# Scan pass of a state-space and attention kernel: a fourth exp buffer, other queue ranks, two states handed over

## The chip, the cores and the metric

The kernel runs on one core of one Trainium2 chip. The metric is the time of one launch on the device in microseconds (us). Its engines work side by side: TensorE (PE, with its weight loads as PEld), VectorE (DVE), ScalarE (ACT), GpSimd (POOL), and SyncE (SP), which here only issues DMAs.

## What is computed

Input x has 8 batches of 64 x 64 positions with 96 channels. A first layer normalizes groups of channels, projects to 2 x 192 channels, convolves one half (3 x 3 by channel, then silu), and runs a selective scan over the 4096 positions in four directions; the result is normalized, gated and projected back. A linear attention and a small quantized feed-forward layer follow. The change touches the selective scan alone:

```python
def step(h, inps):
    d_t, u_t, b_t, c_t = inps
    h = h * jnp.exp(d_t[..., None] * A) + (d_t * u_t)[..., None] * b_t[:, :, None, :]
    y = jnp.einsum('bkdn,bkn->bkd', h, c_t)
    return (h, y)
h0 = jnp.zeros(u.shape[:3] + (A.shape[-1],), u.dtype)
_, ys = jax.lax.scan(step, h0, (dT, uT, BT, CT))
```

For every batch b, direction k (4) and channel d (192) there are 16 states n, each of them a first-order recurrence over 4096 positions, with factor exp(delta A) and addend (delta u) B. The output is the sum over n of h C.

## The kernel before

There are three passes: `pass1` (normalization, projection, convolution, the projections that give delta, B and C), `pass2` (the scans), and `pass3` (all the rest). Intermediate results lie in DRAM between them. The change is in `pass2`, lines 541 to 864.

**Tiling of the scan pass.** Batches go in 4 pairs. The 2 x 192 channels of a pair make three chunks of 128 partitions: chunks 0 and 1 hold 128 channels of one batch each (one-batch chunks, c below 2), and chunk 2 holds the last 64 channels of both (the mixed chunk). Each chunk runs through 4 directions k, and each direction in 4 pieces of 1024 positions (backward for k of 2 and 3). That makes 4 x 3 x 4 x 4 = 192 pieces, each with 16 states: 3072 scans.

**What one piece needs.** `prepare` loads the split factors (`xdt`, `xb`) and `u`, turns B so that it can scale by partition (`bT`), makes `delta` by a softplus on ScalarE, `du` = delta u on GpSimd, and its transpose `duT`. Three of these steps hold a buffer of `wide` (PSUM) for a while. Then for each state n:

- `decay`: ScalarE computes `da` = exp(delta A), 128 x 1024.
- The addend reaches PSUM (`wide`) in one of three ways, chosen by `WAYS` on line 55. ScalarE's way (`scaled`): ScalarE multiplies the 8 blocks of `duT` by B into `x`, in 8 instructions (16 in the mixed chunk), and PE transposes them into `wide`. GpSimd's way (`scaled_by_pool`): the same product in one or two instructions into `xg`. VectorE's way (the rest of the states): PE broadcasts B into `wide` and VectorE multiplies `wide` by `du` in place.
- `scan`: VectorE runs the recurrence over 1024 positions into `h`, which holds two states.
- For each pair of states: `load_c` loads C, broadcast over the partitions, into `c`; `times_c` multiplies `c` by `h` on GpSimd; `sum_over_n` adds the product into `acc` (PSUM) by 16 PE transposes; `carries` copies the last position for the next piece.
- `take_acc` copies `acc` out once all 16 states are in.

**Order.** `weave` (line 142) fixes the order of the instructions on every engine before anything runs. Each unit of work is a generator that yields the engine that it needs next, an estimated cost and a delay, and at times a buffer that must be free. `weave` takes, step after step, the unit that could begin first; among those that could begin at the same time, as is the rule on an engine with a queue, the smaller rank goes first. `add` sets the rank to `at * N + n - lead`: a unit with lead 5 counts as though it belonged five states earlier. `prep` has lead 8. The emitted order is then kept by the hardware's in-order queues, whatever the real times are: an instruction that waits holds up all behind it on its engine.

**Buffers.** `room` (line 550) gives the number of buffers of each kind: 6 of `c`, 3 of `da`, 3 of `h` (pairs of states), 3 of `x`, 3 of `wide`, one each of `xg`, `ud` and `acc`. A `Slots` object for each tells `weave` when the next becomes free by its own estimates. On the chip a semaphore makes the writer wait for it.

Of the kernel before, what the change touches and what calls it, by code (L numbers as in the profile page):

```python
# [51 lines left out]
NPC = L // T  # L52
NT = T // P

WAYS = [([2, 5, 6, 8, 11, 12, 14, 15], [3, 7]), ([2, 3, 7, 9, 14], [0, 5, 12])]
NS = 3

LATE = 5
# [9 lines left out]
def chunk_rows(pair, c):  # L68

    b0 = 2 * pair  # L70
    if c < 2:
        return [(slice(0, P), b0 + c, slice(0, P))]
    return [(slice(64 * j, 64 * j + 64), b0 + j, slice(P, DI)) for j in range(2)]
# [468 lines left out]
def pass2(ctx, tc, g, ident, engines, fixed, u_d, xd_d, b_d, dt_d, y_d):  # L542
# [4 lines left out]
    sp = InOrder(tc, nc.sync)  # L547
    one = ctx.enter_context(tc.tile_pool(name="p2one", bufs=1))
    two = ctx.enter_context(tc.tile_pool(name="p2two", bufs=2))
    room = {"c": 6, "da": 3, "h": 3, "x": 3, "wide": 3, "xg": 1, "ud": 1, "acc": 1}  # L550
    slots = {name: Slots(count) for name, count in room.items()}
    pools = {
        name: ctx.enter_context(tc.tile_pool(name=f"p2{name}", bufs=count, **({"space": PSUM} if name in ("wide", "acc") else {})))
# [7 lines left out]
    def take(name, shape, dtype=F32):  # L561

        return pools[name].tile(shape, dtype, name=name), slots[name].taken
# [79 lines left out]
    def load_c(at, m):  # L643
        pair, c, k, pc = pieces[at]
        parts = chunk_rows(pair, c)
        end = yield "sp", 0.5 * len(parts), 6.0, slots["c"]
        c2, slot = take("c", [P, 2, T])
        row = C0 + (k // 2) * N + 2 * m
        for part, b, _ in parts:
            rows = xd_d[b][k % 2][row : row + 2, pc * T : (pc + 1) * T]  # L650
            sp.dma_start(c2[part], rows.unsqueeze(0).to_broadcast([part.stop - part.start, 2, T]))
        made["c", at, m] = c2, slot
        done["c", at, m] = end

    def decay(at, n):

        _, c, k, _ = pieces[at]
        yield "delta", at
        end = yield "act", 1.06, 0.2, slots["da"]
        da, slot = take("da", [P, T])  # L660
        act.activation(da, made[at][2], AF.Exp, scale=a_neg[:, c // 2, k, n : n + 1])
        made["da", at, n] = da, slot
        done["da", at, n] = end

    def scaled(at, n):

        pair, c, _, _ = pieces[at]
        yield "duT", at
        x, (_, _, _, _, duT, bT) = None, made[at]
        for i in range(0, NT, 2):  # L670
            cost = 0.6 if c < 2 else 1.0
            end = yield ("act", cost, 0.2) if i else ("act", cost, 0.2, slots["x"])
            if i == 0:
                x, slot = take("x", [P, NT, P])
            for i2 in (i, i + 1):
                for j, (part, _, _) in enumerate(chunk_rows(pair, c)):
                    act.mul(x[:, i2, part], duT[:, i2, part], bT[:, i2, j * N + n : j * N + n + 1])
        made["x", at, n] = x, "x", slot
        done["x", at, n] = end

    def scaled_by_pool(at, n):
        pair, c, _, _ = pieces[at]
        yield "duT", at
        end = yield "pool", 2.0 if c < 2 else 2.2, 0.2, slots["xg"]
        x, slot = take("xg", [P, NT, P])
        _, _, _, _, duT, bT = made[at]
        for j, (part, _, _) in enumerate(chunk_rows(pair, c)):
            wide = part.stop - part.start
            b = bT[:, :, j * N + n : j * N + n + 1].to_broadcast([P, NT, wide])
            pool.tensor_mul(x[:, :, part], duT[:, :, part], b)  # L690
        made["x", at, n] = x, "xg", slot
        done["x", at, n] = end

    def products(at, n):

        pair, c, _, _ = pieces[at]
        by_act, by_pool = WAYS[c // 2]
        if n in by_act or n in by_pool:
            yield "x", at, n
            end = yield "pe", 1.3, 0.2, slots["wide"]  # L700
            dbu, slot = take("wide", [P, T])
            x, name, of_x = made["x", at, n]
            for i in range(NT):
                pe.transpose(dbu[:, i * P : (i + 1) * P], x[:, i, :], ident)
            slots[name].release(of_x, end)
        else:
            yield "du", at
            end = yield "pe", 0.7, 0.2, slots["wide"]
            dbu, slot = take("wide", [P, T])
            xb = made[at][0]  # L710
            for q in range(0, T, GRP):
                pe.matmul(dbu[:, q : q + GRP], spread(n, c), xb[:, q : q + GRP], start=True, stop=True)
            end = yield "dve", 1.22, 0.0
            dve.tensor_mul(dbu, made[at][3], dbu)
        made["dbu", at, n] = dbu, slot
        done["dbu", at, n] = end

    def scan(at, n):
        _, _, k, _ = pieces[at]
        rev, first = k >= 2, at % NPC == 0  # L720
        yield "dbu", at, n
        yield "da", at, n
        if not first:
            yield "carry", at - 1, n // 2
        if n % 2 == 0:
            end = yield "dve", 2.26, 0.2, slots["h"]
            made["h", at, n // 2] = take("h", [P, 2, T])
            done["begun", at, n // 2] = 0.0
        else:
            yield "begun", at, n // 2  # L730
            end = yield "dve", 2.26, 0.2
        h = made["h", at, n // 2][0][:, n % 2, :]
        (da, of_da), (dbu, of_dbu) = made["da", at, n], made["dbu", at, n]
        way = slice(None, None, -1) if rev else slice(None)
        init = 0.0 if first else carry[at // NPC][:, n : n + 1]
        dve.tensor_tensor_scan(h[:, way], da[:, way], dbu[:, way], init, ALU.mult, ALU.add)
        slots["da"].release(of_da, end)
        slots["wide"].release(of_dbu, end)
        one_more(("h", at, n // 2), 2, end)
        one_more(("scans", at), N, end)  # L740

    def carries(at, m):

        _, _, k, _ = pieces[at]
        yield "h", at, m
        end = yield "act", 0.12, 0.1
        if at // NPC not in carry:
            carry[at // NPC] = two.tile([P, N], F32, name="carry")
        h2, slot = made["h", at, m]
        last = 0 if k >= 2 else T - 1  # L750
        act.copy(carry[at // NPC][:, 2 * m : 2 * m + 2], h2[:, :, last])
        done["carry", at, m] = end
        one_more(("read", at, m), 2, end)
        if ("read", at, m) in done:
            slots["h"].release(slot, end)

    def times_c(at, m):
        yield "h", at, m
        yield "c", at, m
        end = yield "pool", 4.55, 0.2  # L760
        (h2, slot), (c2, _) = made["h", at, m], made["c", at, m]
        pool.tensor_mul(c2, c2, h2)
        done["term", at, m] = end
        if at % NPC == NPC - 1:
            slots["h"].release(slot, end)
            return
        one_more(("read", at, m), 2, end)
        if ("read", at, m) in done:
            slots["h"].release(slot, end)
# [42 lines left out]
    def take_acc(at):  # L812
        pair, c, k, pc = pieces[at]
        o = k % 2
        yield "sum", at
        end = yield "act", 0.95, 0.1
        if at % (K * NPC) == 0:
            for i in range(2):
                ys[i] = one.tile([P, NBLK, P], F32, name=f"y{i}")
        acc, slot = made["acc"]  # L820
        dst = ys[o][:, pc * NT : (pc + 1) * NT, :]
        act.copy(dst, acc)
        slots["acc"].release(slot, end)
        if k >= 2 and at % NPC == NPC - 1:
            yield "sp", 2.0, 6.0
            store_y(ys[o], o, chunk_rows(pair, c))
# [12 lines left out]
    for at, (pair, c, k, pc) in enumerate(pieces):  # L839
        by_act, by_pool = WAYS[c // 2]  # L840

        def add(kind, lead, unit, n=0):
            units.append((kind, at * N + n - lead, unit))

        add("prep", 8, prepare(at))
        for n in range(N):
            if n % 2 == 0:
                add("c", 12, load_c(at, n // 2), n)
            add("da", 2, decay(at, n), n)
            if n in by_act:  # L850
                add("x", 5, scaled(at, n), n)
            elif n in by_pool:
                add("xg", 4, scaled_by_pool(at, n), n)
            add("dbu", 1, products(at, n), n)
            add("scan", 0, scan(at, n), n)
            if n % 2 == 1:
                if at % NPC < NPC - 1:
                    add("carry", -2, carries(at, n // 2), n)
                add("term", 0, times_c(at, n // 2), n)
                add("sum", -4, sum_over_n(at, n // 2), n)  # L860
        add("acc", 0, take_acc(at), N)
# [289 lines left out]
```

## Time and profile before

| | |
|---|---|
| median of 3 runs | 10227.74 us (10223.3 to 10242.83) |
| the profiled execution's own time | 10238.11 us |
| its span, first to last instruction | 10236.3 us |
| first start and last end of the scans in it | 715.0 and 9321.7 us |
| VectorE busy over the span | 9578.9 us (94%) |
| GpSimd busy | 9194.7 us (90%) |
| ScalarE busy | 9152.3 us (89%) |
| products with C on GpSimd | 1536 x 4.555 us |
| mean granted TensorE clock | 0.895 |

The shares over the whole span mix three passes; the scan pass takes 84% of it. Lines of groups read: source line, engine, operation, output<-inputs with shapes and count, then busy us, mean ns of one, and the engine's idle time just before them with what ended it. Nearly all work goes through one helper, so the source line is L91 throughout and the tile names tell the groups apart: `x` are ScalarE's products, `da` the exps, `h` the scans, `wide` the PSUM buffers.

### The profile page before, as it was taken

The numbers are of one execution on the slowest core, as the hardware profiler recorded it, in microseconds if no ns is written. First come the engines' busy times: TensorE is split into PE (matmuls) and PEld (weight loads), VectorE is DVE, ScalarE is ACT, GpSimd is POOL, SyncE is SP. The second block draws the span as 40 slices with busy tenths as digits, with TensorE's granted clock in tenths as the row PEclk, the third lists the DMA queues.
The fourth block names the chain that finished last, engine by engine and source line by source line (L and its number), as shares of the span: only waits on it lengthen the run. The fifth ranks groups of instructions, "written<-read, shape, count | busy, mean of one in ns | idle before, by whom it ended". The sixth has DMA issues, their size and how long they took to land.

```text
span 10236.3 us, 152471 instructions
## 1 busy us (share of the span) xinstructions
PE 7669.6 (75%) x52384; PEld 6320.8 (62%) x52384; DVE 9578.9 (94%) x6886; ACT 9152.3 (89%) x20499; POOL 9194.7 (90%) x3280
## 2 busy tenths in 40 slices
PE   7767777776777777777777777777777777776887
PEld 3336666665666666666666666666666666565775
DVE  7969999999999999999999999999999999996776
ACT  5669999999999999999999999999999999995665
POOL 1449999999999999999999999999999999997886
PEclk8889989989998989989989999999999899997776
DMA  5766776689976766799866666999667668996442
GB/s 165 236 209 217 229 228 221 228 209 206 211 221 212 224 218 216 223 205 205 221 210 223 219 214 225 209 204 213 216 213 230 210 226 210 206 208 169 125 126 60
DMA packets 928006, 2103.29 MB, mean 205 GB/s; under 512 B 274475, under 2 KB 422732, under 8 KB 925698
## 3 DMA queue, kind: packets, MB, share of 16 engines
q1 hardware_dynamic: 924426, 2092.18, 72.3%
q8 instruction: 420, 6.88, 0.3%
q14 instruction: 352, 2.88, 0.1%
q0 software_dynamic: 432, 0.94, 0.0%
q10 hardware_dynamic: 2376, 0.40, 0.0%
HBM read 1917.59 MB, written 175.66 MB: 204 GB/s over the span
## 4 chain that ended last, share of the span: by engine, by line
DVE 28%; ACT 26%; issue 15%; PE 15%; POOL 12%; DMA 3%; SPq 1%; DVEq 0%; ACTq 0%; POOLq 0%
DVE h L91 20%; ACT x L91 10%; ACT da L91 10%; POOL c L91 8%; PE acc L91 6%; DVE wide L91 5%; PE wide L91 3%; ACT L91 2%; PE mm L91 2%; PE px L91 1%; ACT y L91 1%; POOL xg L91 1%; PE pa L91 1%; DMA xd_d<-xd 1%; ACT delta L91 1%
## 5 line engine op out<-in xcount | busy, mean ns | idle before, releaser
L91 POOL TENSOR_TENSOR c<-c,h 128x2048 f32<-128x2048 f32 x1536 | 6958.0, 4555 | 299.2 <-issue 135.9
L91 DVE TENSOR_TENSOR_SCAN h<-da,carry,wide 128x1024 f32<-128x1024 f32 x2304 | 5268.2, 2332 | 137.6 <-PE wide L91 34.4
L91 ACT ACTIVATE x<-duT,bT 128x128 f32<-128x128 f32 (+1 forms) x13312 | 3970.3, 368 | 2.0
L91 PE MATMUL acc<-ident,c 128*128 128x128 f32 x24576 | 3438.8, 298 | 573.1 <-POOL c L91 566.2
L91 ACT ACTIVATE da<-delta,a_neg 128x1024 f32<-128x1024 f32 x3072 | 3513.1, 1144 | 315.2 <-DVE h L91 302.3
L91 PEld LDWEIGHTS acc<-ident,c 128*128 128x128 f32 x24576 | 3122.8, 155 | 1008.2 <-POOL c L91 893.7
L91 PE MATMUL wide<-ident,x 128*128 128x128 f32 x10752 | 1559.8, 291 | 646.4 <-DVE h L91 587.9
L91 PEld LDWEIGHTS wide<-ident,x 128*128 128x128 f32 x10752 | 1307.2, 150 | 841.5 <-ACT x L91 397.4
L91 DVE TENSOR_TENSOR_SCAN h<-da,wide 128x1024 f32<-128x1024 f32 x768 | 1712.8, 2271 | 45.1 <-PE wide L91 13.9
L91 DVE TENSOR_TENSOR wide<-du,wide 128x1024 f32<-128x1024 f32 x1280 | 1544.2, 1208 | 39.8 <-PE wide L91 29.4
L91 PE MATMUL wide<-xb,sel 96*128 96x512 bf16 x2560 | 820.6, 404 | 696.0 <-DVE h L91 689.1
L91 POOL TENSOR_TENSOR xg<-duT,bT 128x512 f32<-128x512 f32 (+1 forms) x640 | 893.8, 1412 | 28.4 <-PE wide L91 15.3
L91 PEld LDWEIGHTS <-sel 96*128 96x128 bf16 x2560 | 232.8, 102 | 876.4 <-DVE h L91 625.9
L91 PE MATMUL wide<-ident,xg 128*128 128x128 f32 x3584 | 482.6, 279 | 119.0 <-DVE h L91 117.4
L91 PEld LDWEIGHTS wide<-ident,xg 128*128 128x128 f32 x3584 | 411.7, 144 | 148.7 <-issue 110.0
L91 ACT ACT_TABLE_LOAD x385 | 494.0, 1283 | 6.9
L91 POOL TENSOR_TENSOR du<-delta,u 128x1024 f32<-128x1024 f32 x192 | 457.3, 2382 | 7.7 <-DMA u<-u_d 7.7
L91 DVE SCALAR_TENSOR_TENSOR u<-xpad,conv_w,u 128x4096 f32<-128x4096 f32 x96 | 452.7, 4716 | 1.9
L91 PE MATMUL px<-u,w_xp 128*128 128x512 f32 x512 | 253.6, 636 | 61.9 <-ACT u L91 43.0
L91 PE MATMUL mm<-w_out,gt 128*128 128x96 f32 (+1 forms) x1024 | 268.3, 383 | 32.7 <-POOL gt L91 16.1
L91 ACT COPY y<-acc 128x1024 f32<-128x1024 f32 x192 | 192.5, 1003 | 84.5 <-PE acc L91 84.1
L91 POOL TENSOR_TENSOR bq<-bq,bs 128x512 f32<-128x512 f32 (+1 forms) x48 | 121.7, 2536 | 161.4 <-ACT bs L91 140.3
(136 smaller groups left out, 6285.6 us busy)
## 6 DMA issues: line engine op xcount, KB each, us to landing
c<-xd_d SPq DMA_DIRECT2D x1024, 1024.0 KB
c<-xd_d SPq DMA_DIRECT2D x1024, 512.0 KB
u<-u_d SPq DMA_DIRECT2D x127, 512.0 KB
xdt<-dt_d SPq DMA_DIRECT2D x1146, 36.0 KB
xb<-b_d SPq DMA_DIRECT2D x382, 96.0 KB
u<-u_d SPq DMA_DIRECT2D x128, 256.0 KB
y_d<-y SPq DMA_DIRECT2D x24, 1024.0 KB
y<-y_d SPq DMA_DIRECT2D x64, 384.0 KB
```

What stands on the lines that cost most here:

```text
L91: ins = getattr(self.engine, op)(*args, **kwargs).ins
```

## The change

Five values in the scan pass differ; no function is rewritten, and no instruction is added or dropped.

```diff
-WAYS = [([2, 5, 6, 8, 11, 12, 14, 15], [3, 7]), ([2, 3, 7, 9, 14], [0, 5, 12])]
+WAYS = [([2, 5, 6, 8, 10, 13, 14, 15], [3, 7]), ([2, 3, 7, 9, 14], [0, 5, 12])]
...
-    room = {"c": 6, "da": 3, "h": 3, "x": 3, "wide": 3, "xg": 1, "ud": 1, "acc": 1}
+    room = {"c": 6, "da": 4, "h": 3, "x": 3, "wide": 3, "xg": 1, "ud": 1, "acc": 1}
...
             if n % 2 == 0:
-                add("c", 12, load_c(at, n // 2), n)
-            add("da", 2, decay(at, n), n)
+                add("c", 8, load_c(at, n // 2), n)
+            add("da", 0, decay(at, n), n)
             if n in by_act:
-                add("x", 5, scaled(at, n), n)
+                add("x", 8, scaled(at, n), n)
             elif n in by_pool:
                 add("xg", 4, scaled_by_pool(at, n), n)
```

In the one-batch chunks ScalarE's way takes states 10 and 13 in place of 11 and 12, so VectorE's way takes 0, 1, 4, 9, 11, 12 in place of 0, 1, 4, 9, 10, 13. The mixed chunk keeps its split. `da` gets a fourth buffer of 128 x 1024 floats. In the order, loads of C count as 8 states early in place of 12, exps as 0 in place of 2, and ScalarE's products as 8 in place of 5.

## The prediction

> **What bounds the kernel now.** I first read the busy time of each engine by stage, then the waits of VectorE and of ScalarE inside the scan pass, then the groups of instructions, and last the timeline of one stall. The stages come from the first and last start of the scans, 715 us and 9322 us.
>
> The busy time by stage (columns: stretch and length, then busy us and count of PE, PEld, DVE, ACT, POOL, granted clock, DMA share, GB/s):
>
> ```profile
> 0.00:715.00 715.00, 521.22 (x1470) 246.82 (x1470) 548.06 (x244) 432.70 (x588) 231.28 (x110) 0.86 0.67 202
> 715.00:9322.00 8607.00, 6410.87 (x46792) 5484.31 (x46793) 8394.28 (x4351) 8193.57 (x18759) 8283.75 (x2403) 0.92 0.77 215
> 9322.00:10236.30 914.30, 737.48 (x4124) 589.72 (x4122) 636.57 (x2293) 526.00 (x1153) 679.65 (x769) 0.70 0.40 114
> ```
>
> All that the change touches lies in the middle row. There VectorE is busy 8394 of 8607 us (97.5%), GpSimd 96.2%, ScalarE 95.2%. VectorE is the bound, but with only 213 us of idle time, and two engines follow within 200 us. The gain is capped, and a loss is near.
>
> The waits of VectorE in that stage (who waited for whom, us in all, times, longest):
>
> ```profile
> DVE h L91 <- PE wide L91: 48.3, 48, 3.8
> DVE wide L91 <- PE wide L91: 29.4, 30, 1.1
> DVE h L91 <- POOL c L91: 5.3, 6, 1.2
> DVE h L91 <- ACT x L91: 4.6, 5, 2.5
> DVE h L91 <- ACT da L91: 2.1, 3, 1.1
> ```
>
> The long waits sum to some 91 us. The other 120 us are gaps of 0.11 us, 1038 of which stand where a scan follows directly on the multiplication that made its input. The reader is to see that exp (da) holds VectorE up for 2 us in all, so the fourth buffer removes next to no wait of the bound engine. Two thirds of the long waits are for PE. By VectorE's timeline 56 of the 91 us stand at states 9 to 12 of the one-batch chunks (c below 2), and only some 17 us in the mixed chunk.
>
> The waits of ScalarE in the same stage:
>
> ```profile
> ACT da L91 <- DVE h L91: 302.3, 530, 3.3
> ACT y L91 <- PE acc L91: 69.0, 99, 1.4
> ```
>
> ScalarE waits 302 us for a free exp buffer, that is for VectorE: it is often ahead as far as its buffers let it. That time is slack and no cost.
>
> The groups that price the parts (busy us, mean ns of one, idle before and its releasers):
>
> ```profile
> L91 DVE TENSOR_TENSOR_SCAN h<-da,carry,wide 128x1024 f32<-128x1024 f32 x2304 | 5268.2, 2332 | 137.6 <-PE wide L91 34.4
> L91 ACT ACTIVATE x<-duT,bT 128x128 f32<-128x128 f32 (+1 forms) x13312 | 3970.3, 368 | 2.0
> ...
> L91 ACT ACTIVATE da<-delta,a_neg 128x1024 f32<-128x1024 f32 x3072 | 3513.1, 1144 | 315.2 <-DVE h L91 302.3
> ...
> L91 DVE TENSOR_TENSOR wide<-du,wide 128x1024 f32<-128x1024 f32 x1280 | 1544.2, 1208 | 39.8 <-PE wide L91 29.4
> ...
> L91 ACT ACT_TABLE_LOAD x385 | 494.0, 1283 | 6.9
> ```
>
> One typical stall, on VectorE's timeline (start, length, idle before):
>
> ```profile
> 5927.54 2.29 DVE L91 TENSOR_TENSOR_SCAN h<-da,wide 128x1024 f32<-128x1024 f32 x1
> 5930.96 1.23 DVE L91 TENSOR_TENSOR wide<-du,wide 128x1024 f32<-128x1024 f32 x1 [1.13 <-PE wide L91]
> ```
>
> States 9 and 10 both go VectorE's way (broadcast by PE, multiplication, scan). At just this point the next piece's preparation holds one of the three PSUM buffers, so state 10's broadcast waits until state 9's scan has ended, and VectorE stands 1.13 us.
>
> **What the Trainium skill says.** "Perfetto Trace Analysis", section Optimization Strategy, has one look at the gaps of the saturated engine alone, and says that the same gap repeating there can mean too little SBUF or PSUM for the next tile. The 1.13 us gap, repeated at state 10 in some 20 pieces, agrees; but the buffer that is short is the PSUM one, and the change gives exp another. "ScalarE: Activation LUTs", section What ACT_TABLE_LOAD costs, gives about 1283 ns for a table load and an overlap of about 93 ns between ACTIVATEs. The trace agrees with both: 1283 ns, and products of 0.39 us that start 0.295 us apart. So ScalarE's costs in queue time are 8 x 0.295 = 2.4 us for one state's products in a one-batch chunk, 16 x 0.24 = 3.9 us in the mixed one, and 1.144 - 0.1 = 1.04 us for an exp.
>
> **The change, part by part.** Counts of instructions stay as they are: 8 states by ScalarE, 2 by GpSimd and 6 by VectorE in a one-batch chunk before and after, the same loads, the same PE work. Only order and buffers move.
>
> C's loads, lead 12 to 8: SP issues 8 times a piece and mostly waits for one of 6 buffers, so its order is set by when a buffer is free rather than by rank. The other loads of that queue are those of preparation (6 of xdt, 2 of xb, 1 or 2 of u), which could be taken sooner. No wait of VectorE or GpSimd names C's load with more than 5 us. I take 0, and plus or minus 20 us for the ends.
>
> Fourth exp buffer: it takes nothing off VectorE directly (2.1 us). It raises ScalarE's reserve by one exp, that is by one scan of 2.3 us (3.5 us with a multiplication). Cover for other losses, 0 by itself.
>
> Other states by ScalarE (10 and 13 in place of 11 and 12): the neighbouring pair on VectorE's way moves from 9, 10 to 11, 12. The pair's stall of 38 us (25 at state 10, 13 at state 12), with the rest of the 56 us, can go. What is late next is state 10's products: eight transposes by PE take 1.06 us where the broadcast took 0.6, and need the same PSUM buffer. If they wait for state 9's scan too, the stall is 1.3 us in place of 1.13. Also, 13, 14 and 15 are now three ScalarE states in a row: 3 x 2.4 = 7.2 us of products for 3 x 2.3 = 6.9 us of scans. I take half the 56 us as a gain of 28; the ends are -56 and +20.
>
> Ranks: before, products went ahead of an exp only when at most two states beyond it; now they do up to seven states beyond. So ScalarE fills all three product buffers before it returns to exps. Where exps are thinnest is measured: from the end of an exp to the start of its scan there are 4 to 6 us (median) at most states, but 0.8 to 1.2 us at state 12 of the one-batch chunks, just behind the softplus of the next piece. The new order puts there state 15's products (2.4 us) and the preparation (0.25 + 1.28 + 1.11 + 1.28 = 3.9 us) in one stretch of 6.3 us without an exp. With two exps in hand when state 9 begins, VectorE has 1.2 + 2.35 + 2.3 + 1.2 = 7.1 us of work up to state 11's scan, and the exp for that is ready at 6.3 + 1.04 = 7.3: a stall of 0.2 us and the semaphore's way. With three in hand nothing stalls; with one, the stall is some 2.4 us. Queued behind a late exp on ScalarE are the carries, the copy of y and the next products. I take 0.5 us in each of the 128 one-batch pieces, +64 us; the ends are 0 and 128 x 2.4 = 307. In the mixed chunk ScalarE has 3 us idle in each piece of 46, and I take 0 to 60, +5 as a value.
>
> Sum: -28 + 64 + 5 + 0 = +41 us on the profiled execution's 10238.1 us: 10279. The profiled execution lies 10.4 us over the median of the runs shown (10227.7), so the forecast for the median is 10269.
>
> **The rivals.**
> First, the other side: faster. The four exps carry VectorE over the softplus, the pair 11, 12 gives ScalarE 3.5 us for each state just when it has least time, and the 56 us of waits at states 9 to 12 go. For it: ScalarE has 302 us of slack to build the reserve from, and state 15's products, which now end only 0.4 to 1.0 us (median) from the time the scan starts, come earlier. Against it: the exp's own waits are only 2 us, and nothing shortens PE's queue or adds PSUM. Time 10228 - 56 = 10172. It decides from the point where three exps or more are in hand at state 9.
> Second, no change: VectorE's 8394 us are untouched, the stalls only move from state 10 to others, and each engine's order shuffles. Time 10228.
> Third, ScalarE becomes the bound of the one-batch chunks: products ordered that far ahead wait on ScalarE's in-order queue for a product buffer that PE, itself held by GpSimd's terms, frees late, with exps stuck behind. Today products wait 2.0 us in all, which speaks against it. Price up to 2.4 us a piece, 307 us; at two thirds of it, 10430.
>
> **How the numbers follow.** Forecast (a small loss by late exps, own range 10245 to 10350): 0.38. Faster: 0.35. No change: 0.15. ScalarE as bound: 0.12. The two slower cases make 0.50. About 0.2% (20 us) is what a measurement of this kernel can tell from no change. The range 10165 to 10390 takes in the faster case almost whole (its best, with the small gaps, is near 10150) and the third rival's lower half.
>
> **What would show it.** Right: VectorE waits for exp (ACT da) of tens of us where it was 2, at states 10 to 12 of the one-batch chunks; ScalarE's 302 us of waits for an exp buffer well down; waits for PE at state 10 halved. Wrong: VectorE's waits for exp stay near 2 us and its idle time in the pass falls under 190 us (the faster rival); or exps' waits are unchanged and PE's stay near 78 us (no change); or products show tens of us of idle time before them (the third). The prediction falls if GpSimd's idle time instead grows and VectorE waits on it for a state buffer (h), which I priced at nothing.

## The result, and the profile after

The changed kernel takes 10378.11 us (median of 4 runs, 10372.25 to 10388.06) against 10231.85 us for the kernel before in the same runs: ratio 1.0145, 95% interval 1.013 to 1.016. It is 146 us slower, where the forecast was 41.

The profiled executions have spans of 10374.0 and 10236.3 us, 138 us apart. The busy time by stage of the changed kernel (columns as before) puts all of it into the scan pass:

```profile
0.00:712.00 712.00, 520.90 (x1470) 245.20 (x1470) 548.45 (x243) 433.28 (x587) 227.56 (x110) 0.87 0.68 203
712.00:9472.30 8760.30, 6365.35 (x46792) 5454.53 (x46793) 8411.20 (x4351) 8183.63 (x18761) 8293.13 (x2402) 0.93 0.75 212
9472.30:10374.00 901.70, 728.43 (x4124) 579.80 (x4122) 636.63 (x2293) 525.62 (x1153) 678.67 (x769) 0.72 0.40 116
```

The scan pass is 8760.3 us long where it was 8607, so 153 us longer; the last pass is 13 us shorter. VectorE is busy 17 us more, and the rest is idle time: summed over its instructions in the pass it rose from 212 to 349 us. The gaps of some 0.11 us behind a multiplication are about as many as before (1028, 1036 before). What grew are the long waits, over 0.2 us each: 91 us before, 223 us now. The waits of VectorE in the scan pass of the changed kernel (who waited for whom, us, times, longest) say for whom:

```profile
DVE h L91 <- PE wide L91: 158.2, 136, 2.4
DVE wide L91 <- PE wide L91: 23.2, 27, 3.3
DVE h L91 <- ACT carry L91: 18.1, 8, 2.6
DVE h L91 <- ACT delta L91: 9.7, 7, 1.5
DVE h L91 <- ACT x L91: 8.9, 8, 2.2
DVE h L91 <- ACT da L91: 4.0, 4, 1.2
```

The scans' waits for PE rose from 48 to 158 us. Waits for an exp (da) are 4 us, where 2 were. The waits put down to ScalarE's carry and delta all stand at state 10, the place of most of those for PE; a wait for several semaphores is put down to the one that came last in the records. By the state whose multiplication or scan waits, the 223 us are: 105 us (59 waits) at state 10 of the one-batch chunks, 62 us (78 waits, 69 of them at state 14) at states 13 to 15, 22 us at 9, 11 and 12, 4 us at the others, and 29 us in the mixed chunk. Before, state 10 had 26 us (25 waits) and states 13 to 15 had 12.

The waits of ScalarE in the same stage:

```profile
ACT duT L91 <- PE wide L91: 207.2, 103, 3.8
ACT carry L91 <- DVE h L91: 179.5, 219, 3.1
ACT da L91 <- DVE h L91: 128.4, 154, 3.3
```

ScalarE waits less for a free exp buffer (128 us for 302), but more at other places: it is ahead, and waits for what the others have not finished. It is not the engine that is late. From the start and end times, an exp is ready 4.7 to 9.4 us (median by state) before its scan at states 10 to 13 of the one-batch chunks, and at state 12, where it was 0.8 to 1.2 us, 8.7 to 9.4.

One stall at state 10, from the timeline of the changed kernel (start, length, engine, work, idle before it):

```profile
5425.76 0.24 ACT L91 COPY bT<-wide 128x128 f32<-128x128 f32 x1
...
5425.82 0.59 PE L91 MATMUL wide<-xb,sel 96*128 96x512 bf16 x2 [1.39 <-DVE h L91]
...
5427.92 1.21 DVE L91 TENSOR_TENSOR wide<-du,wide 128x1024 f32<-128x1024 f32 x1
5428.05 0.59 PE L91 MATMUL wide<-xdt,dt_w 108*128 108x512 bf16 x2
...
5429.23 2.35 DVE L91 TENSOR_TENSOR_SCAN h<-da,carry,wide 128x1024 f32<-128x1024 f32 x1
...
5431.72 1.94 PE L91 MATMUL wide<-ident,x 128*128 128x128 f32 x8 [3.08 <-DVE h L91]
...
5433.80 2.35 DVE L91 TENSOR_TENSOR_SCAN h<-da,carry,wide 128x1024 f32<-128x1024 f32 x1 [2.22 <-PE wide L91]
```

Read it from below. State 10's scan waits 2.22 us for the eight transposes of its products. Those start at 5431.72, when state 9's scan (5429.23 + 2.35) ends, and PE has then stood idle for 3.08 us. Yet a buffer of `wide` has been free since 5426.0, when ScalarE had copied B's transposed values (bT) out of it. The addresses in the emitted program tell why PE didn't use it: state 10's transposes write the buffer that was handed out two times before, to state 9, and not the one three times before, which was bT's.

That is how `wide` is handed out. The planner's `Slots` reckon that three buffers go round strictly in turn. The pool that gives out the addresses doesn't keep to a turn. In 58 of the 128 one-batch pieces of the changed kernel, and in 23 before, it gives state 10 the buffer of two times before, the one that state 9's scan is still to read. The waits at state 10 number 59 and 25, and every one of the 58 and of the 23 pieces has its wait. What makes the pool choose so in one piece and not in the next is not shown: the copy of bT stands in the emitted program behind the start of state 10's PE work in all of the 58 and the 23, but also in 10 and 27 of the other pieces. The experiments below use this count.

The waits at states 13 to 15 carry the same mark one step earlier. In 103 of the 128 pieces of the changed kernel PE's work for state 13 was given the buffer that state 11's scan had still to read, though another of the three (the one that the softplus reads) came free at least 3.3 us sooner, 5.5 us in the median. Of the 69 waits at state 14, 66 are in these pieces. By this count PE falls behind at state 13 and VectorE meets it one state later; no run takes this step apart from state 10's.

### The profile page after: what moved, and what is told of

It is laid out like the page before. It is cut to its first block, busy times and chain, and to the rows that moved or that the text cites. A ratio compares the mean times of both kernels' runs of the same rounds, so it can differ in the third digit from the quotient of the medians.

```text
span 10374.0 us, 152498 instructions
## 1 busy us (share of the span) xinstructions
PE 7614.7 (73%) x52384; PEld 6279.5 (61%) x52384; DVE 9596.3 (93%) x6886; ACT 9142.5 (88%) x20499; POOL 9199.4 (89%) x3280
## 4 chain that ended last, share of the span: by engine, by line
ACT 29%; DVE 28%; PE 14%; issue 14%; POOL 7%; DMA 1%; SPq 0%; DVEq 0%; POOLq 0%; ACTq 0%
DVE h L91 20%; ACT x L91 13%; ACT da L91 11%; PE acc L91 6%; DVE wide L91 6%; PE wide L91 5%; POOL c L91 4%; PE mm L91 2%; ACT y L91 1%; ACT duT L91 1%; ACT L91 1%; POOL gt L91 1%; DMA c<-xd_d 1%; PE tr L91 0%; POOL xg L91 0%
## 5 line engine op out<-in xcount | busy, mean ns | idle before, releaser
L91 PEld LDWEIGHTS wide<-ident,x 128*128 128x128 f32 x10752 | 1282.0, 149 | 1558.3 <-ACT x L91 648.2
L91 PE MATMUL wide<-xb,sel 96*128 96x512 bf16 x2560 | 780.4, 394 | 406.0 <-DVE h L91 375.4
L91 ACT COPY duT<-wide 128x1024 f32<-128x1024 f32 x192 | 193.1, 1006 | 207.6 <-PE wide L91 207.2
L91 ACT COPY carry<-h 128x2 f32<-128x2 f32 x1152 | 211.5, 184 | 183.9 <-DVE h L91 179.5
L91 PE MATMUL mm<-w_out,gt 128*128 128x96 f32 (+1 forms) x1024 | 259.9, 373 | 35.5 <-POOL gt L91 15.4
```

The costliest lines, as they stand in the source:

```text
L91: ins = getattr(self.engine, op)(*args, **kwargs).ins
```

## The experiments

Three theories. A: the loss is this hand-out. PE is given a buffer that a scan still holds while another lies free; which edit brings it about is a matter of the emitted order. B, the recorded forecast: exps are late because products go ahead of them. C: the new split of states is the loss by itself.

**One edit at a time.** The split alone:

```diff
-WAYS = [([2, 5, 6, 8, 11, 12, 14, 15], [3, 7]), ...
+WAYS = [([2, 5, 6, 8, 10, 13, 14, 15], [3, 7]), ...
```

> Only the new split of states (10 and 13 by ScalarE), all else as before. Theory A (the loss is PE work for state 10 that is given the PSUM buffer state 9's scan is still reading; in the emitted program that holds for 58 of the 128 one-batch pieces of the changed kernel, for 23 before, and for 23 here): state 10's waits some 23 x 1.5 = 35 us where they were 25, plus up to 54 us at state 14, if that belongs to three ScalarE states in a row: +10 to +65 us, ratio 1.001 to 1.006. Theory B (as predicted: exps late because of the ranks): the split alone gives -28 us, ratio 0.997, at most +20. Theory C (the split is the whole loss): +146 us, ratio 1.0145.

Measured: 10269.28 us, ratio 1.0038 (1.0025 to 1.0051). State 10 has 35 waits with 52 us, states 13 to 15 have 18 us. C falls: the split makes about a quarter of the loss. B's gain of 28 us isn't there either.

The ranks alone:

```diff
-add("da", 2, ...    add("x", 5, ...
+add("da", 0, ...    add("x", 8, ...
```

> Only the ranks of exp (0) and of ScalarE's products (8), three exp buffers, old split. A: state 10 takes the buffer of the running scan in 13 pieces only (23 before): ratio 0.997 to 1.003, VectorE's waits for PE no more than before. B: with three exp buffers late exps are worse than in the changed kernel: VectorE waits 64 us or more for exp, ratio over 1.006. C: 1.000.

Measured: 10272.63 us, ratio 1.0042 (1.0027 to 1.0057). This missed A's range, and B's as well. State 10 has only 13 us, as A has it, but the loss comes by another way. VectorE's waits in the scan pass of this run:

```profile
DVE wide L91 <- PE wide L91: 59.1, 76, 1.1
DVE h L91 <- PE wide L91: 42.6, 44, 2.9
DVE h L91 <- ACT da L91: 12.2, 22, 1.3
```

The third line is B's mechanism: with three exp buffers and the new ranks, exps do come late, but that costs 12 us and not 64. The first line is larger: 59 us of multiplications waiting for PE's broadcast, where the kernel before had 29. So the ranks alone cost waits for PE too, and 42 us of them (55 waits) stand before state 13's multiplication, where the kernel before had one. In all 55 the broadcast was given the buffer of state 11's scan, which runs just ahead of that multiplication, though another had come free at least 2.7 us sooner. That is the mark of the hand-out at another state than the one that A had counted; this kernel was not run with the buffers in turn.

The fourth exp buffer alone:

```diff
-room = {"c": 6, "da": 3, ...
+room = {"c": 6, "da": 4, ...
```

> Only the fourth exp buffer. A: 14 such pieces at state 10: ratio 0.996 to 1.001, ScalarE's waits for an exp buffer below 302 us. B: nothing or a small gain, 0.998 to 1.000. C: 1.000.

Measured: 10207.77 us, ratio 0.9979 (0.997 to 0.9987), a gain of 21 us. The long waits fall to 66 us. ScalarE's waits in that run:

```profile
ACT da L91 <- DVE h L91: 145.1, 244, 3.3
ACT carry L91 <- DVE h L91: 120.3, 243, 2.1
```

The wait for an exp buffer is halved, and most of what was taken off comes back as waits for the scan whose end is to be carried.

**The change with one edit undone.** The old split:

```diff
-WAYS = [([2, 5, 6, 8, 10, 13, 14, 15], [3, 7]), ...
+WAYS = [([2, 5, 6, 8, 11, 12, 14, 15], [3, 7]), ...
```

> The changed kernel with the old split of states. A: 22 such pieces at state 10 in place of 58, and no three ScalarE states in a row, so nearly the whole loss goes: ratio 0.998 to 1.004. B: the ranks stay, so a loss of 64 us or more stays: 1.006 or more. C: 1.000, as in A; A and C differ in the run with the split alone.

Measured: 10214.63 us, ratio 0.9987 (0.998 to 0.9994): faster than before. The ranks with four exp buffers lose nothing as long as states 11 and 12 stay with ScalarE; B falls here. With the split alone at 1.0038, neither the split nor all the rest without it makes the loss of 1.0145.

Three exp buffers:

```diff
-room = {"c": 6, "da": 4, ...
+room = {"c": 6, "da": 3, ...
```

> The changed kernel with three exp buffers. In the emitted program 26 of the one-batch pieces have state 10's PE work on the buffer of the running scan, against 58 with four. A: some 26 x 1.8 = 47 us at state 10 in place of 105, so 1.006 to 1.011. B: with one exp fewer in hand exps come later, over 1.015.

Measured: 10318.25 us, ratio 1.0093 (1.0079 to 1.0106). State 10 has 32 waits with 59 us. So the fourth buffer, a gain of 21 us by itself, adds some 50 us of loss beside the other two edits. The waits for an exp in this run are 15.4 us, again far below the 64 of the forecast.

The old ranks of exp and products:

```diff
-add("da", 0, ...    add("x", 8, ...
+add("da", 2, ...    add("x", 5, ...
```

> The changed kernel with the old ranks of exp and products (2 and 5); the split, the fourth exp buffer and C's lead stay. The emitted program has 22 such pieces at state 10. A: some 40 us at state 10, 1.001 to 1.006. If split and buffer suffice for the loss: 1.012 or more.

Measured: 10276.33 us, ratio 1.0051 (1.0036 to 1.0067), 51 us of waits at state 10 and 14 us at states 13 to 15. With the new split, the 62 us at 13 to 15 thus come with the new ranks: this run and the split alone have 14 and 18 us there, while the run with split, ranks and three exp buffers has 52.

The old lead of C's loads:

```diff
-add("c", 8, ...
+add("c", 12, ...
```

> The changed kernel with the old lead of 12 for C's loads. All theories: the lead orders next to nothing; 58 pieces at state 10 as in the changed kernel: ratio 1.013 to 1.016.

Measured: 10380.55 us, ratio 1.0151 (1.0136 to 1.0167). The lead of C's loads does nothing that can be measured.

**The hand-out itself.** This takes the suspected cause away and leaves the rest: same instructions, in the same order on each engine of the emitted program, three pools of one buffer each in place of one pool of three, taken in turn as the planner counts.

```diff
-        for name, count in room.items()
+        for name, count in room.items() if name != "wide"
     }
+    turn = [ctx.enter_context(tc.tile_pool(name=f"p2wide{i}", bufs=1, space=PSUM)) for i in range(room["wide"])]
...
-        return pools[name].tile(shape, dtype, name=name), slots[name].taken
+        taken = slots[name].taken
+        pool_of = turn[taken % room["wide"]] if name == "wide" else pools[name]
+        return pool_of.tile(shape, dtype, name=name), taken
```

On the changed kernel:

> The changed kernel with the three PSUM buffers handed out strictly in turn (three pools of one buffer each, taken by the planner's own count), so that state 10's PE work gets the buffer that B's transposed values left long before. Order of every engine by the planner is the same. A: the 105 us of waits at state 10 go, other states may lose some: ratio to before 1.002 to 1.007. B: exps are as late as before the edit, no change: 1.0145. If the hand-out is as good as a strict turn elsewhere, the gain is all at state 10.

Measured: 10238.91 us, ratio 1.0009 (1.0002 to 1.0015). Of the 146 us, 10 are left (10238.91 against 10228.78 us for the kernel before in the same runs); more went than A said. No long wait is left at state 10, and states 13 to 15 fall from 62 to 17 us. At state 0, 27 us have come up, so that the long waits sum to 80 us. The same place of the same piece, on the timeline of this run:

```profile
5352.38 0.24 ACT L91 COPY bT<-wide 128x128 f32<-128x128 f32 x1
...
5354.69 0.59 PE L91 MATMUL wide<-xdt,dt_w 108*128 108x512 bf16 x2
5355.12 1.04 PE L91 MATMUL wide<-ident,x 128*128 128x128 f32 x8
...
5355.86 4.59 DVE L91 TENSOR_TENSOR_SCAN h<-da,carry,wide 128x1024 f32<-128x1024 f32 x2
```

State 10's transposes start at once behind the preparation's multiplication, before state 9's scan has begun, and the scans of states 9 and 10 run as one block of 4.59 us. VectorE's waits in its scan pass:

```profile
DVE h L91 <- PE wide L91: 44.8, 35, 2.3
DVE wide L91 <- ACT x L91: 17.2, 29, 1.2
DVE wide L91 <- PE wide L91: 12.0, 20, 2.1
```

The scans' 158 us for PE are down to 45. This shows A: only the hand-out was altered, and the loss is gone but for 10 us. The edit takes every buffer of `wide` in turn, so the shares of state 10 and of the other states are not separated by it.

On the kernel before:

> The kernel before with the three PSUM buffers handed out strictly in turn. A: 23 waits of 1.13 us at state 10 go (25 us), at most the 56 us at states 9 to 12: ratio 0.994 to 0.999. B and C say nothing on it: 1.000. If the free hand-out helps elsewhere: above 1.000.

Measured: 10194.09 us, ratio 0.9965 (0.9952 to 0.9977). One long wait of 0.5 us is left at state 10, and the long waits sum to 50 us in place of 91. So the kernel before paid for the hand-out as well.

**Versions that beat both.** The kernel before in turn, with the fourth exp buffer:

> The kernel before with the PSUM buffers handed out in turn and the fourth exp buffer. If the two gains (0.9965 by the turn, 0.9979 by the fourth buffer) come from different waits they add up: 0.994 to 0.9955. If the fourth buffer helped only because it shifted the hand-out (14 collisions at state 10 in place of 23), nothing is left of it: 0.9955 to 0.9975.

Measured: 10178.19 us, ratio 0.9954 (0.9941 to 0.9966), long waits of 46 us. The interval holds both answers, so it stays open whether the fourth buffer's own gain adds to the turn's in full.

The changed kernel in turn, with the old split:

> The changed kernel with the old split and the buffers in turn. Without it the old split gave 0.9987, with 21 us of waits at state 10, which go: 0.995 to 0.9975.

Measured: 10171.32 us, ratio 0.9947 (0.9934 to 0.9959), a little better than expected and the lowest time of all, though its interval overlaps that of the run above. Its long waits are 49 us. It keeps the fourth buffer and all the new ranks. With the hand-out in turn in both, the old split is 68 us faster than the new one (10171.32 against 10238.91; each against its own runs of the kernel before, 0.9947 and 1.0009). So the new split loses time beside these ranks even without the fault of the hand-out; 22 us of it are the waits at state 0 (27 against 4 us), the rest was not taken apart.

## Why the prediction was right in sign and wrong in cause

**The number and the sign.** 10378 lies within the stated range of 10165 to 10390, but beyond the 10245 to 10350 that the forecast gave its own mechanism. What holds it is the room left for ScalarE as the bound, which did not come. That the range holds, and that the sign is right, is luck: the one large positive term stood for a wait that stayed at 4 us. Of the signs named for being right, ScalarE's waits for an exp buffer did fall; the waits for exps did not grow to tens of us, and the waits at state 10 were not halved but grew fourfold (26 to 105 us). GpSimd's idle time grew too, from 323 to 467 us of the pass, but VectorE did not wait for it.

**The bound.** Right. VectorE bounds the scan pass before and after, and the change in time is its change in idle time plus 17 us of busy time. Nine of the eleven variants stay within 0.6% of the kernel before, as a gain capped by 91 us of waits and a loss close at hand would have it.

**C's loads, taken at 0.** Right, within the interval.

**The fourth exp buffer, "Cover for other losses, 0 by itself".** Too small: alone it gains 21 us. The argument that exps hold VectorE up for only 2 us was true, but not enough. A longer reserve on ScalarE also changes the planned order of everything behind it; with this buffer alone, 14 pieces give state 10 the scan's buffer, where 23 did.

**The split, taken at -28 us with ends of -56 and +20.** This is the step that failed. The text had the very case, "If they wait for state 9's scan too, the stall is 1.3 us in place of 1.13", and priced it as a larger wait in as many pieces as before. Instead the number of pieces went from 25 to 59 and the wait to 1.8 us (105 / 59): +79 us at state 10, and with states 13 to 15 +129, with all edits together. The split alone measured +41 us, twice its upper end. Pieces with and without the stall stood side by side in the profile of before. What set them apart was a buffer that the planner didn't choose, and it was never looked for. In the very stall that the prediction shows, one of the three was free (before, ScalarE and PE):

```profile
5926.13 0.24 ACT L91 COPY bT<-wide 128x128 f32<-128x128 f32 x1
...
5929.89 1.04 PE L91 MATMUL wide<-xb,sel 96*128 96x512 bf16 x2 [0.74 <-DVE h L91]
```

bT's buffer was free from 5926.37; the broadcast was given state 9's and started when that scan had ended.

**The ranks, taken at +64 us by late exps.** Wrong. Exps hold VectorE up for 4 us in the changed kernel, 12 us with the ranks alone, and 15 us with split and ranks on three buffers. The error is in the sum of 6.3 us without an exp against 7.1 us of work. It lets the stretch without an exp begin together with state 9, with two exps in hand, so that state 11 waits. In the traces the stretch begins 2.1 us (median) after state 9's multiplication has begun, and lasts 5.0 us in the changed kernel and 5.6 us in the two runs with the new ranks on three buffers. The first exp behind it is state 13's in 121 of the 128 pieces of the changed kernel, ready 5.1 us ahead of its scan; on three buffers it is mostly state 12's, ready 1.3 us (ranks alone) or 2.1 us (split and ranks) ahead. Alone, the ranks cost 44 us, not far from the 64, but for the wait for PE. The ranks do take part in the loss, but by the counts of buffers through the hand-out: with the buffers in turn and the old split they stand in the fastest version (0.9947).

**The mixed chunk, taken at +5.** +18 us of long waits (29 for 12).

**The sum.** Measured one at a time, split, ranks and fourth buffer come to 41 + 44 - 21 = +64 us. The other 82 of the 146 us are there only with the edits together, which a sum of separate terms can't hold.

**Readings of the profile before.** Some were off. PE ended 78 of the 92 us in the table of VectorE's waits, not two thirds. The mixed chunk has 12 us of long waits, not 17. An exp lay 4 to 6 us ahead of its scan (median) at seven of the sixteen states, not at most of them, and state 15's products on ScalarE ended 2.4 to 3.2 us ahead of its scan, not 0.4 to 1.0. No large term of the sum rests on these.

**The rivals.** Faster by the going of the waits at states 9 to 12: what it asked of ScalarE came true (exps long in hand), but the waits moved into PE's buffer. ScalarE as the bound: its products waited 3.4 us in all, so no. No change fails on the number. The forecast's sum of +41 was low because its one large positive term was for the wrong engine, and the term that came stood in it with a minus.

**The Trainium skill.** The section Optimization Strategy of "Perfetto Trace Analysis", that a repeating gap on the saturated engine can point to a buffer, led to the right place. The prediction even named PSUM as the buffer that is short. But there was none too few: the same three, handed out in turn, end the gap at state 10.

## What to carry to other kernels

When a planner orders the work by its own count of buffers, read in the emitted program which buffer each write really gets: a write whose buffer an instruction just running still reads is a hidden wait, even if another buffer lies free. Where a stall comes in some repeats of a loop and not in others, find out what sets them apart before a price is put on it. Edits to order and buffers need not add up: the fourth buffer was a gain alone and a loss beside the new split and ranks, so each is to be measured in the setting in which it will stay.

## What had not been expected of the hardware

Eight PE transposes took either some 1.06 us or 1.94 us. In the changed kernel, of 155 such groups behind more than 2.9 us of idle time on PE, 66 took over 1.4 us, and 56 of these began while the records show a granted clock of 0.5. Of 335 groups behind 1 to 2 us of idle time 46 took as long, and of 541 without idle time before or within them 23. At state 10 the stall is larger for it: 30 waits of over 1.9 us (67 us in all), with all or nearly all of the eight transposes at a granted clock of 0.5, and 29 below (39 us), none of whose groups began at 0.5. Whether the idle time itself lowers the clock, no run here shows.

A scan that directly follows the multiplication which made its input starts 0.11 us after it (1038 such gaps, 119 us in the kernel before), where two scans one behind the other overlap by 0.08 us. A scan behind a multiplication for another state overlaps it by 0.09 us (212 such pairs), so the gap goes with the need for the result and not with the change of operation.
